# First masks of an attention layer made beside the layer before, three late tiles, and parts between two kinds of matmul

## The chip, the core and the metric

The kernel runs on one core of a Trainium2 chip. A core has five engines with an instruction queue each: TensorE (PE in the profile: matmuls and transposes, with its weight loads shown apart as PEld), VectorE (DVE), ScalarE (ACT), GpSimd (POOL) and SyncE (SP, which here only starts transfers). Each engine works through its queue in the order in which the program issued to it, and waits where an instruction needs something that is not there yet. The metric is the time of the whole program on the device in microseconds, the median of several runs.

## The reference

There are 2708 nodes with 256 features, `x`, and a matrix `adj` of 2708 x 2708. Two layers follow each other, each ending in x = layernorm(x + layer(x)).

```
# layer 0, S = adj
R = S + I, its rows scaled to sum 1
for n in 0, 1:                       # Xf = Xa = X at the start
    A  = top_p_attention(Xa)         # softmax of bilinear scores, kept to 0.9 of its mass
    Xf = R @ Xf ;  Xa = A @ Xa
    Z += Xf @ U1[n].T + Xa @ U2[n].T
layer0 = layernorm(X + Z) * ln_g + ln_b

# layer 1, 4 heads of 64
Wh  = x @ W[h]
e   = leaky_relu(s_i + s_j, 0.2)     # s_i, s_j: Wh with two vectors per head
att = softmax over j of e where adj != 0 or i == j
layer1 = att @ Wh, heads side by side
```

## The kernel before, in words

The nodes are cut into 22 tiles: tiles 0 to 15 have 128 rows, tiles 16 to 21 have 110. All matmuls are in float32.

**Layer 0** (`fast_layer0`) goes through the tiles twice (`step`, s = 0 and 1). For each target tile t, `weigh` turns the attention weights `e` in six groups of up to four tiles (`turned`: transposes by TensorE into a PSUM tile `tr`, a copy by ScalarE into `eT`) and multiplies them with the values into the PSUM tile `att`. After each group `between` is called. It scales the result into `xa` after the last group (L1030), and it calls `slot`, which lets the generators that are under way go on by one part each: the search for the kept weights of a later tile (`search`, mostly VectorE), the walk with `adj` (`walks`, TensorE, L901, with blocks `blk` of `adjT` in three buffers of `adjp`), and `finish`. In the second step `finish(t)` collects the terms of a tile (L974 on VectorE, L976 on ScalarE, L979 to L982 on GpSimd); then `norms` makes the two layernorms and `sources` what layer 1 needs of the tile as a source: transposes (L160), a copy, a matmul with the layer's weights (L166), and by ScalarE the exponentials `sb` and `tj` and the values `cs`, which are stored to DRAM as `vd[t]`. In `norms`, L129 to L137 are `layernorm` on VectorE, with the power -1/2 on GpSimd (L135); the multiplication with `g_sb` and the addition of `xt` (L187, L188) are GpSimd's.

The last four tiles, 18 to 21 (`LATE = 4`), end late, and layer 1 does not need them at once as sources. Their norms and sources are left to layer 1: the generator `prepared(t)`, which uses `layernorm_beside` (L145 to L153): three ScalarE passes and four small GpSimd operations for each norm.

**Layer 1** (`layer1`) takes the target tiles in three groups (`spans`: 8, 8 and 6 tiles, that is 1024, 1024 and 660 targets). For each group all 22 source tiles j are gone through in pairs; in the first group in the order `first`: 8 to 17, 0 to 7, 18 to 21. For one source tile

- `mask` starts the load of `v[j]` (only in the first group, L1290) and calls `neighbours`: a block of `adjT` (up to 128 x 1024) is fetched by SP into one of the three buffers of `adjp`, ScalarE makes zeros and ones of it with two passes (Sign, L1221, and Square, L1222), and where j is among the group's targets VectorE sets the diagonal (L1225);
- `weights` makes four products by VectorE, one for each head (`pt`, L1302), from the targets' terms, `tj` and the mask; there are three sets of buffers for them (`DEEP = 3`);
- `values` multiplies them with `v` into four PSUM accumulators (L1313), and `denominators` with `sb` into two more (L1323).

The loop runs over pairs of source tiles. For each it calls, in this order: `beside`, `weights` and `mask` of a later tile, `values` of both tiles, `denominators` of both, `beside` again (not in a group's last pair), `weights` and `mask` of another later tile. This order is the order of the engines' queues; SP alone is ordered by the framework. `beside` lets each late part go on by one step: the four `prepared` generators, started two calls apart, then `verdict` (checks of the fast path, some 20 small VectorE operations), then the parts of the last group's results (`settle`). At i = 11 it shares the next group's target terms.

The line numbers of the profile are those of this kernel.

Of the kernel before, what the change touches and what calls it, by code (L numbers as in the profile page):

```python
# [44 lines left out]
def kernel(  # L45
# [68 lines left out]
    g_sb = const.tile([P, D], F32, name="g_sb")  # L114
    b_sb = const.tile([P, D], F32, name="b_sb")

    LATE = 4
    x_late = const.tile([P, LATE, D], F32, name="x_late")
    engines = {nc.tensor.engine, nc.scalar.engine, nc.vector.engine, nc.gpsimd.engine}

# [57 lines left out]
            )  # L178
        queue.dma_start(vd[t][:m], vt[:m])  # L179

    def norms(t, xt, norm=layernorm, other=None):

        m = rows[t]
        hh = xe[:m, t, 0:D]
        h2 = hh if other is None else other()[:m]
        yield from norm(h2, hh, m)
        nc.gpsimd.tensor_mul(h2, h2, g_sb[:m])  # L187
        nc.gpsimd.tensor_add(h2, h2, xt[:m])  # L188
        yield
        yield from norm(hh, h2, m)  # L190
        yield
        if t < NT - LATE:
            yield

    GT = 8
    spans = [list(range(g, min(g + GT, NT))) for g in range(0, NT, GT)]
# [20 lines left out]
    def spread(g, r):  # L217

        lines = shared[g].rearrange("(t h) m -> h t m", h=H)
        n = len(spans[g]) * rows[spans[g][0]]  # L220
        for k in range(2):
            for h in range(2):
                nc.sync.dma_start(
                    r[k][:, h, :n].rearrange("p (t m) -> p t m", t=len(spans[g])),
                    lines[2 * k + h].partition_broadcast(P),
                )

    def room(pool):

# [295 lines left out]
    def fast_layer0(ep, adjp):  # L525
# [461 lines left out]


        going, doing, unfinished, stored = [], [], set(), set()
        ready, held = {}, {}  # L990
        stream = walks()
        owed = [0]
# [17 lines left out]
                    break  # L1010

        def step(s, cur, spend):
            first = None
            for t in range(NT):
                m = rows[t]
                e, rden = ready[t]
                ac = ps_at.tile([P, CHUNK], F32, name="att")
                if s == 0 and t == NT - 1:
                    next(stream)
                if s and t == NT - 2:  # L1020
                    share(0, ps_tr.tile([P, 4, P], F32, name="tr"))
                if s and t == NT - 1:
                    ahead.extend(room(ep))
                    spread(0, ahead)

                def between(n):
                    last = n == len(groups) - 1
                    if last:
                        xa = heldp.tile([P, D], F32, name="xa1")
                        nc.scalar.activation(xa[:m], ac[:m, :D], AF.Copy, scale=rden)  # L1030
                        if s and t in c3:
                            nc.gpsimd.dma_start(c3[t][:m], xa[:m])
                            stored.add(t)
                        elif s:
                            held[t] = xa
                        else:
                            doing.append(after_attention0(t, xa))
                    slot(spend[n], (s, t + 3) if n == len(groups) - 2 else None)

                def turn_next(n):  # L1040
                    u = t + n // len(groups)
                    if u == NT:
# [3 lines left out]
                first = weigh(  # L1046
                    ac[:m, :D], first or turn_next(0), m,
                    lambda j: cur[: rows[j], j, 0:D], turn_next, between,
                )
                ready.pop(t)  # L1050
# [131 lines left out]
            )  # L1182

        l0.close()
        return ahead, verdict

# [1 line left out]

    def layer1(ep, adjp, r=None, verdict=None):
        l1 = ExitStack()

        pp, rp, pj, keep = (
# [7 lines left out]
        first = list(range(GT, NT - LATE)) + list(range(GT)) + list(range(NT - LATE, NT))  # L1204


        v = {}
        for t in reversed(first):
# [1 line left out]

        def aux():
            return ps_u.tile([P, H, P], F32, name="aux")

        def neighbours(g, j):

            k = rows[j]
            i0, i1 = off[spans[g][0]], off[spans[g][-1] + 1]
            bar = adjp.tile([P, NT - HT, P], F32, name="blk")
            bar = bar.rearrange("p t d -> p (t d)")[:k, : i1 - i0]
            nc.sync.dma_start(bar, adjT[off[j] : off[j + 1], i0:i1])  # L1220
            nc.scalar.activation(bar, bar, AF.Sign)  # L1221
            nc.scalar.activation(bar, bar, AF.Square)  # L1222
            if j in spans[g]:
                own = bar[:, off[j] - i0 : off[j + 1] - i0]
                nc.vector.tensor_tensor(own, own, ident[:k, :k], op=ALU.max)  # L1225
            return bar

        def settle(g, t, val, den, u, last):

# [56 lines left out]
        def mask(n):  # L1286
            if n < len(order):
                g, _, j = order[n]
                if g == 0:
                    nc.scalar.dma_start(  # L1290
                        v[j][: rows[j]].rearrange("p h o -> p (h o)"), vd[j][: rows[j]]
                    )
                masks[n] = neighbours(g, j)

        def weights(n):
            if n < len(order):
# [32 lines left out]

        def prepared(t):  # L1330

            yield from norms(
                t, x_late[:, t - NT + LATE, :], layernorm_beside,
                lambda: pp.tile([P, D], F32, name="h2", bufs=4),
            )
            yield from sources(t, pp, aux, nc.scalar)


        late = []
        if verdict:  # L1340
            late += [[2 * k, prepared(NT - LATE + k)] for k in range(LATE)]
            late.append([2 * LATE, verdict(aux)])
        rest, running = [], []
        def beside(g, i):

            for part in list(late):
                if part[0] > 0:
                    part[0] -= 1
                elif next(part[1], late) is late:
                    late.remove(part)  # L1350
            for part in list(running):
                if next(part, running) is running:
# [17 lines left out]
        for n in range(0, len(order), 2):  # L1370
# [103 lines left out]
```

## Time and profile before

| what | value |
|---|---|
| median of 3 runs | 1587.1 us (1586.86 to 1587.92) |
| the profiled execution's own time | 1586.25 us |
| its span in the profile | 1584.4 us |
| TensorE busy | 1537.4 us, 97% |
| VectorE busy | 1201.2 us, 76% |
| ScalarE busy | 799.5 us, 50% |
| GpSimd busy | 440.9 us, 28% |
| last matmul of layer 0's attention (L258) ends | 1221.1 us from the span's start |
| first matmul of layer 1's values (L1313) begins | 1225.2 us |
| end of the first group of layer 1 (its last L1323) | about 1359.6 us |

A row of the timeline gives the start in microseconds from the span's start, the length, engine, line, operation, the output and inputs by the program's names, their shapes and the number of instructions that were merged; in brackets how long the engine stood idle before it, and what ended that. A `MATMUL` in float32 shows as two instructions. "Busy" of TensorE contains some overlap of matmuls that follow each other, so the distance from one start to the next is the better measure of what a group costs.

### The profile page before, as it was taken

The page shows a single profiled execution, that of the slowest core. Times are in us where ns is not written, and L with a number is a line of the kernel's source. Part 1 is how long each engine was busy: PE and PEld are TensorE (multiplying, and loading weights), DVE is VectorE, ACT ScalarE, POOL GpSimd, SP SyncE. Part 2 cuts the span into 40 slices and gives each one's busy share as a digit, 9 for nine tenths or more (in the row PEclk, how much of TensorE's full clock was granted, in tenths as well). Part 3 has the DMA queues.
Part 4 walks back from the last instruction along what each step waited for, and adds up shares of the span by engine and source line. Part 5 has one row for each costly group of instructions (what it writes and reads, how often), then busy time and mean ns, then how long its engine had stood idle before and what let it go on. Part 6 is the DMA issues. An engine that isn't in the chain of part 4 may idle for free. (4 is left out here: it accounts for less than half of the span.)

```text
span 1584.4 us, 23826 instructions
## 1 busy us (share of the span) xinstructions
PE 1537.4 (97%) x8029; PEld 1036.2 (65%) x8029; DVE 1201.2 (76%) x3651; ACT 799.5 (50%) x1462; POOL 440.9 (28%) x884
## 2 busy tenths in 40 slices
PE   8999999999998999999999999999998989999994
PEld 4477777776776888787778788887786323333342
DVE  4686776777309767877779888888883888999895
ACT  3444444444345455555645566656643454456473
POOL 2200000100023122232223544444541750044133
PEclk9999999999999999999999999999999999999998
DMA  6100000000144333332333444333343335334231
GB/s 163 61 12 13 9 13 9 9 11 11 43 114 105 100 84 102 80 89 72 85 89 95 110 109 109 104 99 93 91 101 110 110 110 161 95 107 133 81 100 43
DMA packets 172495, 128.27 MB, mean 81 GB/s; under 512 B 44342, under 2 KB 161804, under 8 KB 172362
## 3 DMA queue, kind: packets, MB, share of 16 engines
q1 hardware_dynamic: 162000, 111.86, 26.4%
q0 software_dynamic: 3648, 9.26, 1.7%
q10 hardware_dynamic: 6714, 5.54, 1.1%
q8 instruction: 65, 1.06, 0.3%
q14 instruction: 68, 0.56, 0.1%
HBM read 111.78 MB, written 13.46 MB: 79 GB/s over the span
## 5 line engine op out<-in xcount | busy, mean ns | idle before, releaser
L245 ACT COPY eT<-tr 128x512 f32<-128x512 f32 (+5 forms) x264 | 141.3, 535 | 287.5 <-PE tr L240 284.9
L686 ACT ACTIVATE junk<-e,minus,rth 128x2708 bf16<-128x2708 f32 (+1 forms) x88 | 232.8, 2646 | 36.1 <-POOL rth L718 35.2
L258 PE MATMUL att<-xm,eT 128*128 128x256 f32 (+3 forms) x968 | 230.9, 380 | 0.4 <-ACT xa L1030 0.4
L258 PE MATMUL att<-ba,eT 128*128 128x256 f32 (+3 forms) x968 | 230.8, 379 | 0.3 <-ACT eT L245 0.2
L901 PE MATMUL walk<-xe,blk 128*128 128x257 f32 (+3 forms) x968 | 225.3, 384 | 5.0 <-DVE xf L915 5.0
L901 PE MATMUL walk<-xm,blk 128*128 128x256 f32 (+3 forms) x968 | 222.0, 380 | 1.0 <-DVE xw L974 1.0
L1313 PE MATMUL acc<-pt,v 128*64 128x512 f32 (+3 forms) x1056 | 213.7, 548 | 4.5 <-DVE pt L1302 4.1
L901 PEld LDWEIGHTS walk<-xe,blk 128*128 128x128 f32 (+3 forms) x968 | 178.5, 187 | 50.3 <-issue 12.6
L1302 DVE SCALAR_TENSOR_TENSOR pt<-e,tj,blk 128x1024 f32<-128x1024 f32 (+3 forms) x176 | 185.5, 1122 | 20.7 <-ACT blk L1222 16.0
L901 PEld LDWEIGHTS walk<-xm,blk 128*128 128x128 f32 (+3 forms) x968 | 177.7, 186 | 34.4 <-issue 4.9
L258 PEld LDWEIGHTS att<-xm,eT 128*128 128x128 f32 (+3 forms) x968 | 169.6, 186 | 22.1 <-ACT xa L1030 0.8
L258 PEld LDWEIGHTS att<-ba,eT 128*128 128x128 f32 (+3 forms) x968 | 169.5, 186 | 22.0 <-ACT eT L245 0.8
L665 ACT ACTIVATE e<-lg 128x1024 f32<-128x1024 f32 (+1 forms) x132 | 121.0, 921 | 110.6 <-PE lg L661 107.0
L1313 PEld LDWEIGHTS acc<-pt,v 128*64 128x64 f32 (+1 forms) x1056 | 74.7, 137 | 132.9 <-issue 109.4
L766 DVE MAX8 cand<-e 128x8 f32<-128x170 f32 (+1 forms) x352 | 89.6, 324 | 90.5 <-ACT e L665 90.4
L240 PEld LDWEIGHTS tr<-ident,e 128*128 128x128 f32 (+3 forms) x968 | 115.1, 138 | 56.3 <-issue 21.0
L240 PE MATMUL tr<-ident,e 128*128 128x128 f32 (+3 forms) x968 | 147.1, 271 | 0.7 <-ACT xe L952 0.3
L1302 DVE SCALAR_TENSOR_TENSOR pt<-r,tj,blk 128x1024 f32<-128x1024 f32 (+1 forms) x88 | 109.8, 1312 | 6.1 <-PE acc L1323 3.2
L1323 PE MATMUL acc<-pt,sb 128*32 128x512 f32 (+3 forms) x1056 | 106.8, 545 | 0.0
L766 DVE MAX8 cand<-scr 128x8 f32<-128x97 f32 (+1 forms) x616 | 102.3, 246 | 0.0
L915 DVE TENSOR_TENSOR xf<-walk,xe 128x257 f32<-128x257 f32 (+1 forms) x22 | 9.4, 426 | 110.6 <-PE walk L901 110.6
L784 DVE MAX8 top<-work 128x8 f32<-128x128 f32 (+3 forms) x242 | 82.4, 340 | 8.3
(237 smaller groups left out, 1966.9 us busy)
## 6 DMA issues: line engine op xcount, KB each, us to landing
blk<-in_adjT_dram SPq DMA_DIRECT2D x32, 704.0 KB
blk<-in_adjT_dram SPq DMA_DIRECT2D x32, 512.0 KB
blk<-in_adjT_dram SPq DMA_DIRECT2D x48, 330.0 KB
blk<-in_adjT_dram SPq DMA_DIRECT2D x32, 320.0 KB
blk<-in_adjT_dram SPq DMA_DIRECT2D x12, 605.0 KB
blk<-in_adjT_dram SPq DMA_DIRECT2D x12, 440.0 KB
blk<-in_adjT_dram SPq DMA_DIRECT2D x18, 283.6 KB
c<-cs POOLq DMA_DIRECT2D x32, 128.0 KB, 2.0
```

The lines of the kernel that those rows point to most:

```text
L240: nc.tensor.transpose(tr[: rows[t], q, :m], e[:m, off[t] : off[t + 1]], ident[:m, :m])
L245: copy(eT[:k, : len(grp), :m], tr[:k, : len(grp), :m])
L258: nc.tensor.matmul(acc, eT[: rows[t], q, :m], value(t), start=(t == 0), stop=(t == NT - 1),)
L665: nc.scalar.activation(halves[:m, :, c0 : c0 + w], lg[:m, :, :w], AF.Exp, accum_out=zp[:m, n : n + 1],)
L686: nc.scalar.activation(junk[:m], e[:m], func, scale=rth, bias=minus1[:m], accum_out=acc)
L766: nc.vector.max(cand[:, n, :], src[:m, n * size : min(N, (n + 1) * size)])
L784: nc.vector.max(top[:, k : k + 8], work if k else flat)
L901: nc.tensor.matmul(ac[:m, :w], blk[: rows[j], j - j0, :m], cur[: rows[j], j, 0:w], start=(j == 0), stop=(j == NT - 1),)
L915: nc.vector.tensor_add(xf[:m], ac[:m, : D + 1], xe[:m, t, :])
L1302: nc.vector.scalar_tensor_tensor(pt[:k, :gw], targets[g][h // 2][:k, h % 2, :gw], tj[:k, j, h : h + 1], bar, op0=ALU.max, op1=ALU.mult,)
L1313: nc.tensor.matmul(acc[h // 2][c][q * FO : (q + 1) * FO, :w], v[j][:k, h, :], probs[n][h][:k, c0 : c0 + w], **at,)
L1323: nc.tensor.matmul(acc[2][c][h * 32 : (h + 1) * 32, :w], sb[:k, j, h : h + 1].to_broadcast([k, 32]), probs[n][h][:k, c0 : c0 + w], **at,)
```

## The change

- `LATE` is 3: tile 18 is finished in layer 0 like the tiles before it, with `layernorm` on VectorE; `first` becomes 8 to 18, 0 to 7, 19 to 21.
- `norms` serves the early tiles alone. For the three late tiles `prepared` writes its own norms: the statistics, the epsilon, the column `nb` and also the multiplication with `g_sb` and the addition on VectorE, one operation on GpSimd (`pow`), one pass on ScalarE. Two calls of `beside` with nothing to do lie between `pow` and `nb`. One tile takes 12 calls instead of 8.
- `neighbours` moves to the outer function, and in the second step of layer 0, at the last tile after the last but one group, the first two masks of layer 1 are made (`early`). In `mask` they are then taken as they are.
- The loads of the first three `v[j]` are started on SP instead of ScalarE's queue.
- The second call of `beside` in a pair comes between `values` and `denominators`.
- `verdict` starts after 26 calls of `beside` (`NT + 4`) instead of 8, that is in the second group.

```diff
-    LATE = 4
+    LATE = 3
...
-    def norms(t, xt, norm=layernorm, other=None):
+    def norms(t, xt):
 
         m = rows[t]
         hh = xe[:m, t, 0:D]
-        h2 = hh if other is None else other()[:m]
-        yield from norm(h2, hh, m)
-        nc.gpsimd.tensor_mul(h2, h2, g_sb[:m])
-        nc.gpsimd.tensor_add(h2, h2, xt[:m])
+        yield from layernorm(hh, hh, m)
+        nc.gpsimd.tensor_mul(hh, hh, g_sb[:m])
+        nc.gpsimd.tensor_add(hh, hh, xt[:m])
         yield
-        yield from norm(hh, h2, m)
+        yield from layernorm(hh, hh, m)
         yield
-        if t < NT - LATE:
-            yield
+        yield
...
+    first = list(range(GT, NT - LATE)) + list(range(GT)) + list(range(NT - LATE, NT))
+
+    def neighbours(g, j, adjp):
+
+        k = rows[j]
+        i0, i1 = off[spans[g][0]], off[spans[g][-1] + 1]
+        bar = adjp.tile([P, NT - HT, P], F32, name="blk")
+        bar = bar.rearrange("p t d -> p (t d)")[:k, : i1 - i0]
+        nc.sync.dma_start(bar, adjT[off[j] : off[j + 1], i0:i1])
+        nc.scalar.activation(bar, bar, AF.Sign)
+        nc.scalar.activation(bar, bar, AF.Square)
+        if j in spans[g]:
+            own = bar[:, off[j] - i0 : off[j + 1] - i0]
+            nc.vector.tensor_tensor(own, own, ident[:k, :k], op=ALU.max)
+        return bar
...
+                    if s and (t, n) == (NT - 1, len(groups) - 2):
+
+                        early.extend(neighbours(0, j, adjp) for j in first[:2])
                     slot(spend[n], (s, t + 3) if n == len(groups) - 2 else None)
...
-                    nc.scalar.dma_start(
+                    (nc.sync if n < DEEP else nc.scalar).dma_start(
                         v[j][: rows[j]].rearrange("p h o -> p (h o)"), vd[j][: rows[j]]
                     )
-                masks[n] = neighbours(g, j)
+                masks[n] = early[n] if n < len(early) else neighbours(g, j, adjp)
...
         def prepared(t):
 
-            yield from norms(
-                t, x_late[:, t - NT + LATE, :], layernorm_beside,
-                lambda: pp.tile([P, D], F32, name="h2", bufs=4),
-            )
+            m = rows[t]
+            xt = x_late[:m, t - NT + LATE, :]
+            hh = xe[:m, t, 0:D]
+            h2 = pp.tile([P, D], F32, name="h2", bufs=LATE)[:m]
+            for src, dst in ((hh, h2), (h2, hh)):
+                if src is h2:
+                    nc.vector.tensor_mul(h2, h2, g_sb[:m])
+                    nc.vector.tensor_add(h2, h2, xt)
+                st = small.tile([P, 6], F32, name="ln_st")[:m]
+                mv = small.tile([P, 2], F32, name="ln_mv")[:m]
+                ve, rs, nb = (small.tile([P, 1], F32, name=f"ln_{k}")[:m] for k in ("ve", "rs", "nb"))
+                nc.vector.bn_stats(st, src)
+                nc.vector.bn_aggr(mv, st)
+                nc.vector.tensor_scalar(ve, mv[:, 1:2], LN_EPS, None, op0=ALU.add)
+                nc.gpsimd.tensor_tensor(rs, ve, minus_half[:m], op=ALU.pow)
+
+                yield
+                yield
+                yield
+                nc.vector.tensor_scalar(nb, mv[:, 0:1], rs, -1.0, op0=ALU.mult, op1=ALU.mult)
+                yield
+                nc.scalar.activation(dst, src, AF.Identity, scale=rs, bias=nb)
+                yield
             yield from sources(t, pp, aux, nc.scalar)
 
         late = []
         if verdict:
             late += [[2 * k, prepared(NT - LATE + k)] for k in range(LATE)]
-            late.append([2 * LATE, verdict(aux)])
+            late.append([NT + 4, verdict(aux)])
...
+            if not last:
+                beside(g, i + 1)
             for u in (n, n + 1):
                 denominators(u)
             if last:
...
                 rest = [(g, t, val, den) for t in spans[g]]
-            else:
-                beside(g, i + 1)
             weights(n + 3)
             mask(n + 4)
```

`early` is handed from `fast_layer0` to `layer1`; a local variable `first` in `step` is renamed.

More of the change, by code (lines that the diff above doesn't have):

```diff
@@ L989, in fast_layer0 @@
         going, doing, unfinished, stored = [], [], set(), set()
+        early = []
         ready, held = {}, {}
@@ L1012, in step @@
         def step(s, cur, spend):
-            first = None
+            turned_first = None
             for t in range(NT):
@@ L1044, in turn_next @@
                     return turned(ready[u][0], rows[u], n % len(groups), tpp, ps_tr, nc.scalar.copy)
-                first = weigh(
-                    ac[:m, :D], first or turn_next(0), m,
+                turned_first = weigh(
+                    ac[:m, :D], turned_first or turn_next(0), m,
                     lambda j: cur[: rows[j], j, 0:D], turn_next, between,
@@ L1184, in fast_layer0, with layer1 @@
         l0.close()
-        return ahead, verdict
-    def layer1(ep, adjp, r=None, verdict=None):
+        return ahead, verdict, early
+    def layer1(ep, adjp, r=None, verdict=None, early=()):
         l1 = ExitStack()
@@ L1202, in layer1 @@
         ps_v = l1.enter_context(tc.tile_pool(name="ps_v", bufs=1, space=PSUM))
-        first = list(range(GT, NT - LATE)) + list(range(GT)) + list(range(NT - LATE, NT))
         v = {}
@@ L1212, in aux @@
             return ps_u.tile([P, H, P], F32, name="aux")
[L1214 to L1226, printed above, removed]
         def settle(g, t, val, den, u, last):
```

## The prediction, made before the change was built

> **What bounds the kernel now.** I read the shares of busy time first, then the instructions of TensorE in order of time from the end of the last attention, then the other engines over the same stretch, to see what TensorE waits for.
>
> ```profile
> PE 1537.4 (97%) x8029; PEld 1036.2 (65%) x8029; DVE 1201.2 (76%) x3651; ACT 799.5 (50%) x1462; POOL 440.9 (28%) x884
> ```
>
> TensorE is busy for 1537 of 1584.4 us, so only its gaps are to be won. TensorE in order of time (start, length, line, operation, count, idle time before it and who ended it):
>
> ```profile
> 1218.35 2.75 PE L258 MATMUL att<-ba,eT 110*110 110x256 f32 x12
> 1225.22 10.30 PE L1313 MATMUL acc<-pt,v 128*64 128x512 f32 x32 [4.11 <-DVE pt L1302]
> 1235.45 3.64 PE L1323 MATMUL acc<-pt,sb 128*32 128x512 f32 x32
> ...
> 1249.61 9.21 PE L1313 MATMUL acc<-pt,v 128*64 128x512 f32 x32
> ...
> 1273.25 1.14 PE L166 MATMUL aux<-wx,xT 128*110 128x264 f32 x4
> 1276.58 0.41 PE L160 MATMUL aux<-ident,xe 110*128 110x110 f32 x2 [2.19 <-ACT xe L153]
> 1276.92 7.09 PE L1313 MATMUL acc<-pt,v 110*64 110x512 f32 x32
> 1283.94 3.64 PE L1323 MATMUL acc<-pt,sb 110*32 110x512 f32 x32
> 1287.51 1.14 PE L166 MATMUL aux<-wx,xT 128*110 128x264 f32 x4
> 1290.86 0.41 PE L160 MATMUL aux<-ident,xe 110*128 110x110 f32 x2 [2.21 <-ACT xe L153]
> ```
>
> An undisturbed pair of source tiles costs 10.59 us: 7.02 of values and 3.57 of denominators (1276.92, 1283.94, 1287.51). Layer 1 loses time at three kinds of place: 4.11 us before its first matmul, a first pair (10.23 instead of 7.02) and a third pair (9.14) that are too long, and 2.2 us, three times, between a late tile's L166 and the next one's L160 (the third, 2.10, is before L160 at 1305.14). After 1317 TensorE has no such gap until the end. VectorE, ScalarE and GpSimd beside it:
>
> ```profile
> 1223.88 24.01 DVE L1302 SCALAR_TENSOR_TENSOR pt<-e,tj,blk 128x1024 f32<-128x1024 f32 x20 [11.34 <-ACT blk L1222]
> 1251.96 15.39 DVE L1302 SCALAR_TENSOR_TENSOR pt<-e,tj,blk 128x1024 f32<-128x1024 f32 x12 [4.07 <-ACT blk L1222]
> 1267.92 10.59 DVE L1302 SCALAR_TENSOR_TENSOR pt<-e,tj,blk 110x1024 f32<-110x1024 f32 x8 [0.57 <-ACT blk L1222]
> ```
>
> ```profile
> 1218.61 0.34 ACT L245 COPY eT<-tr 110x220 f32<-110x220 f32 x1 [1.39 <-PE tr L240]
> 1221.14 0.47 ACT L1030 ACTIVATE xa<-att,rden 110x256 f32<-110x256 f32 x1 [2.19 <-PE att L258]
> 1221.70 1.06 ACT L1221 ACTIVATE blk<-blk 128x1024 f32<-128x1024 f32 x1
> 1222.79 1.06 ACT L1222 ACTIVATE blk<-blk 128x1024 f32<-128x1024 f32 x1
> ...
> 1248.89 0.60 ACT L153 ACTIVATE h<-xe,lb_nb,lb_rs 110x256 f32<-110x256 f32 x1 [9.39 <-POOL lb_nb L151]
> ```
>
> ```profile
> 1234.98 12.96 POOL L149 TENSOR_SCALAR lb_sq<-lb_sq 110x1 f32<-110x1 f32 x1 [6.13 <-ACT h L148]
> ```
>
> The first product waits for its mask, which ScalarE makes after `xa`. From 1223.88 VectorE makes 20 products at 1.20 us each with no pause: eight per pair, 9.6 us, against TensorE's 10.59, so it has 1 us to spare per pair once level, and in the first pair it is the pace (last values 11.57 after the first product). L149 ends only when that run of VectorE ends; ScalarE's L153 stood behind it, the next mask behind L153: that is the third pair's delay.
>
> **The change, part by part** (against the profiled execution: 1586.25 us, span 1584.4, 0.85 below the median of 1587.1).
>
> *Masks made early.* ScalarE does four mask passes after its last `eT` copy, at 1218.95: the first mask is ready 2 x 1.07 later, at 1221.1, when the last attention matmul ends. The product then starts 2.78 us sooner relative to that end: **-2.8**. Its other needs are there: masks 0 and 1 were fetched at 1195 and 1204, the targets' copies were issued at 1200.5, and by the order and sizes of the pools the first eight products lie where `xm` and `qT` were, last read at 1212.5. The two fetches move ahead in the program but take the same buffers, which the walks free, so SP issues them (0.36 each) when it does now. What queues behind the passes on ScalarE: `xa` slips from 1221.14 to about 1223.2, and with it GpSimd's L981 and L982 (0.72 each), which now run beside products. By the pools' order one accumulator takes `att`'s bank; it is first written 5.3 us after the first product, after `xa`. If a target or buffer is late the gain is nothing: +2.8.
>
> *Three v loads on SP*, 0.3 us of issue each, behind fetches that wait for buffers anyway. The first pair is paced by VectorE, so v may land 2 us late for nothing: 0.
>
> *Tile 18 goes back into layer 0.* TensorE's L160 and L166 cost 0.19 and 0.89 there (start to start at 1180.16 and 1186.35, tile 17), 0.34 and 1.07 in layer 1: **-0.3**. VectorE gains 2 x (0.85 + 0.41) us and a wait for GpSimd of up to 1.5; its idle 4.08 us before L974 at 1195.23 hides that, and `e` of the last tile is ready at 1202.4, 2.2 us before its use: 0, at worst +1.
>
> *Parts between values and denominators.* The next tile's L160 stood right behind L166, waiting for ScalarE (sb, tj, s_src, four cs, a store, L153: 2.14 us). Now 3.57 us of denominators lie between: **-6.5** (2.19 + 2.21 + 2.10). In groups 1 and 2 only `share` changes place on TensorE.
>
> *Norms.* Four GpSimd operations and three ScalarE passes per norm become one GpSimd `pow` and one pass; ScalarE's Identity now follows VectorE's `nb`, three calls after `pow`, so no mask stands behind a late GpSimd: the third pair's delay goes, **-2.1**. VectorE pays: bn_stats, bn_aggr and the epsilon 0.85 (the same three at 1155.09), `nb` 0.2 (as L743, a column by a column, 0.21), multiply and add 0.42 each (as L974). By the product that ends the sixth pair: 48 products at 1.20 = 57.6, six norm starts 5.1, four `nb` 0.8, three multiply-adds 2.5, together 66.0; three matmuls of 0.44 (7.02 us are 16) follow: 67.3 us after the first product. TensorE alone would be there at 11.57 + 3.57 + 4 x 10.59 + 0.34 + 7.02 = 64.9. So VectorE is the bound for the first six pairs: **+2.5**. Afterwards L166 gives it time back.
>
> The unknown is what GpSimd beside it costs. Bounds: 0 (20 products at 1.20 with L146 and L149 in the run) and 7.2 (40 products at 1.32, as the eight at 1267.92, 4.8; four `nb` waiting 0.6 for their `pow`, 2.4). I take **+1.5**, nearest to the 12 products of 15.39 us, where some ten GpSimd operations cost 0.9; here there are eight, two of them wide.
>
> [...]
>
> *Verdict later.* 3.9 us of VectorE move to group 1's third to seventh pair, where VectorE idles 0.4 to 0.8 us per pair and products may be 2.6 late: 0, at worst +1.6.
>
> Sum: -2.8 - 0.3 - 6.5 - 2.1 + 2.5 + 1.5 = **-7.7**, so 1587.1 - 7.7 = 1579.4 us.
>
> **Rivals.**
> A. GpSimd and VectorE hold each other up at the upper bound: 5.7 us dearer, gain 2.0, 1585.1 us. For it: 1.32 us products around 1270. Against: most of GpSimd's work leaves.
> B. The early masks do nothing, because the first product waits for something that the mask hid until now: gain 4.9, 1582.2 us. For it: nothing shows what else ended before 1223.88. Against: the buffers and fetches above.
> C. Slower: GpSimd is shut out as in the L149 of 12.96 us, and VectorE's waiting at `nb` does not let it in. L981 is asked for 2 us after the first product, L982 and the six `pow` queue behind it at p us each, so the last `pow` ends at 2 + 8p; its `nb` is due at 73, with products behind it on VectorE and TensorE behind these. At 12.96 us that is 33 late: 1612.1 us. It costs from p = 8.9 on and makes the kernel slower than before, beyond what can be told, from 10.3 (11 late). For it: one row. Against: that row ended with VectorE's run, and at `nb` VectorE stands still.
>
> **How the numbers follow.** Forecast 0.57, A 0.18, B 0.15, C 0.10. Measurement tells 0.2%, 3.2 us, from no change. Faster by that: the forecast, B and a third of A, 0.78; within it: the rest of A, 0.12; slower: C, 0.10. The forecast's own range is 1577 (no GpSimd cost, some VectorE work in its idle moments) to 1582; with A and B it reaches 1576 to 1586.
>
> **What would show it.** First product within 0.5 us of the last attention matmul's end and TensorE's gap there 1.3 instead of 4.1; no wait before L160; VectorE without a pause from there until about 67 us later, with short waits of TensorE on products in the fourth to sixth pair; `pow` under 2 us or waits at `nb` under 1; VectorE's products in the stretch at 1.20 to 1.25. Wrong it would be by a late target, a GpSimd backlog, or TensorE waiting in layer 0's last tile.

## The result

The changed kernel takes 1575.88 us (median of 4 runs, 1575.84 to 1576.54) against 1587.34 us (4 runs, 1586.86 to 1587.92): 11.5 us less. The ratio is 0.9929, 95% interval 0.9911 to 0.9946. Forecast were 1579.4 us, in a range of 1576.0 to 1586.0.

The profiled execution of the changed kernel took 1576.54 us, its span is 1574.7 us; against the 1584.4 us of before that is 9.7 less. Line numbers move: L1302 is now L1305 (products), L1313 L1316 (values), L1323 L1326 (denominators), L258 L273 (last attention), L1221 and L1222 L236 and L237 (mask passes), L981 and L982 L996 and L997; the new norms are L1341 to L1356.

TensorE in order of time, after (the columns are those of before):

```profile
1220.45 2.76 PE L273 MATMUL att<-ba,eT 110*110 110x256 f32 x12
1225.87 10.07 PE L1316 MATMUL acc<-pt,v 128*64 128x512 f32 x32 [2.66 <-DVE pt L1305]
1235.88 3.64 PE L1326 MATMUL acc<-pt,sb 128*32 128x512 f32 x32
...
1250.03 7.09 PE L1316 MATMUL acc<-pt,v 128*64 128x512 f32 x32
...
1260.62 8.12 PE L1316 MATMUL acc<-pt,v 128*64 128x512 f32 x32
...
1272.24 7.85 PE L1316 MATMUL acc<-pt,v 110*64 110x512 f32 x32
...
1283.93 7.71 PE L1316 MATMUL acc<-pt,v 110*64 110x512 f32 x32
1291.57 1.14 PE L166 MATMUL aux<-wx,xT 128*110 128x264 f32 x4
...
1292.76 3.64 PE L1326 MATMUL acc<-pt,sb 110*32 110x512 f32 x32
1296.33 0.41 PE L160 MATMUL aux<-ident,xe 110*128 110x110 f32 x2
```

The gap ahead of the first values is 2.66 instead of 4.11 us, the third pair takes 7.09 instead of 9.21, and L160 follows without a wait. New are three pairs of 8.12, 7.85 and 7.71 us. VectorE and GpSimd beside it:

```profile
1223.30 10.59 DVE L1305 SCALAR_TENSOR_TENSOR pt<-e,tj,blk 128x1024 f32<-128x1024 f32 x8 [8.68 <-PE att L273]
...
1234.56 9.65 DVE L1305 SCALAR_TENSOR_TENSOR pt<-e,tj,blk 128x1024 f32<-128x1024 f32 x8
```

```profile
1225.57 0.79 POOL L996 TENSOR_TENSOR xe<-xe,xa 110x256 f32<-110x256 f32 x1 [9.27 <-ACT xa L1046]
1226.32 1.70 POOL L997 TENSOR_TENSOR x_late<-x_late,b_sb 110x256 f32<-110x256 f32 x1
1234.72 1.52 POOL L1349 TENSOR_TENSOR ln_rs<-ln_ve,minus_half 110x1 f32<-110x1 f32 x1 [6.69 <-DVE ln_ve L1348]
```

The first product starts 0.09 us after the last attention matmul (2.77 before). The eight products beside L996 and L997 take 1.32 us each, the next eight, beside a `pow`, 1.20.

The two profiled executions side by side, in microseconds:

| stretch | before | after | difference |
|---|---|---|---|
| span's start to the 26th matmul | 13.25 | 13.48 | +0.23 |
| from there to the end of the last attention matmul | 1207.86 | 1209.73 | +1.87 |
| from there to the end of the last matmul | 343.17 | 333.86 | -9.31 |
| from there to the span's end | 20.10 | 17.62 | -2.48 |
| span | 1584.4 | 1574.7 | -9.7 |

The third row is the sum of: first product -2.68, first pair +1.01 (11.57 to 12.58 from first product to last values), third pair -2.12, three waits before L160 -6.50, tile 18's L160 and L166 gone from layer 1 -1.41, pairs four to six +2.41; that makes -9.29. The last row but one was nowhere in my sum.

### The profile page after: what moved, and what is told of

Read it like the earlier page. It is cut to its first block, busy times and chain, and to the rows that moved or that the text cites. A ratio compares the mean times of both kernels' runs of the same rounds, so it can differ in the third digit from the quotient of the medians.

```text
span 1574.7 us, 23765 instructions
## 1 busy us (share of the span) xinstructions
PE 1537.8 (98%) x8029; PEld 1037.3 (66%) x8029; DVE 1207.8 (77%) x3689; ACT 791.7 (50%) x1428; POOL 407.6 (26%) x853
## 4 chain that ended last, share of the span: by engine, by line
PE 92%; DVE 4%; POOL 1%; ACT 1%; issue 1%; DMA 0%; ACTq 0%; POOLq 0%; DVEq 0%
PE att L273 25%; PE walk L916 24%; PE acc L1316 13%; PE lg L676 7%; PE acc L1326 7%; PE tr L255 6%; PE tr L961 2%; PE tr L975 2%; PE tr L646 1%; PE tr L166 1%; DVE scr L766 1%; DVE scr L847 0%; DVE cand L781 0%; DVE e L850 0%; PE aux L1236 0%
## 5 line engine op out<-in xcount | busy, mean ns | idle before, releaser
L273 PE MATMUL att<-xm,eT 128*128 128x256 f32 (+3 forms) x968 | 230.9, 380 | 0.4 <-ACT xa L1046 0.4
L273 PE MATMUL att<-ba,eT 128*128 128x256 f32 (+3 forms) x968 | 230.8, 379 | 0.3 <-ACT eT L260 0.2
L1316 PE MATMUL acc<-pt,v 128*64 128x512 f32 (+3 forms) x1056 | 214.3, 551 | 2.7 <-DVE pt L1305 2.7
L1305 DVE SCALAR_TENSOR_TENSOR pt<-e,tj,blk 128x1024 f32<-128x1024 f32 (+3 forms) x176 | 184.2, 1112 | 12.7 <-PE att L273 8.7
L273 PEld LDWEIGHTS att<-xm,eT 128*128 128x128 f32 (+3 forms) x968 | 169.6, 186 | 22.1 <-ACT xa L1046 0.8
L273 PEld LDWEIGHTS att<-ba,eT 128*128 128x128 f32 (+3 forms) x968 | 169.5, 186 | 22.0 <-ACT eT L260 0.8
L1316 PEld LDWEIGHTS acc<-pt,v 128*64 128x64 f32 (+1 forms) x1056 | 75.7, 138 | 132.0 <-issue 107.8
L1305 DVE SCALAR_TENSOR_TENSOR pt<-r,tj,blk 128x1024 f32<-128x1024 f32 (+1 forms) x88 | 109.8, 1310 | 3.0 <-PE acc L1326 1.3
L1326 PE MATMUL acc<-pt,sb 128*32 128x512 f32 (+3 forms) x1056 | 106.8, 545 | 0.0
L236 ACT ACTIVATE blk<-blk 128x1024 f32<-128x1024 f32 (+3 forms) x66 | 63.3, 958 | 83.5 <-DMA blk<-in_adjT_dram 63.3
```

The lines of the kernel that those rows point to most:

```text
L273: nc.tensor.matmul(acc, eT[: rows[t], q, :m], value(t), start=(t == 0), stop=(t == NT - 1),)
L1305: nc.vector.scalar_tensor_tensor(pt[:k, :gw], targets[g][h // 2][:k, h % 2, :gw], tj[:k, j, h : h + 1], bar, op0=ALU.max, op1=ALU.mult,)
L1316: nc.tensor.matmul(acc[h // 2][c][q * FO : (q + 1) * FO, :w], v[j][:k, h, :], probs[n][h][:k, c0 : c0 + w], **at,)
L1326: nc.tensor.matmul(acc[2][c][h * 32 : (h + 1) * 32, :w], sb[:k, j, h : h + 1].to_broadcast([k, 32]), probs[n][h][:k, c0 : c0 + w], **at,)
```

## The experiments

Every kernel was timed in at least five executions beside the kernel before on the same chip, whose median lay at 1586.7 to 1587.4 us. The stretches of the table above are called seam (last attention matmul to last matmul) and tail (last matmul to the span's end) here. The expectations of the two runs on GpSimd's last branch count the tail from the last matmul's start, which adds 0.3 us. In the code, cuts are marked by `...`.

### The parts behind the denominators again

```diff
-            if not last:
-                beside(g, i + 1)
             for u in (n, n + 1):
                 denominators(u)
             if last:
                 ...
                 rest = [(g, t, val, den) for t in spans[g]]
+            else:
+                beside(g, i + 1)
             weights(n + 3)
```

> The changed kernel with one thing undone: the second round of parts of a pair is called behind the denominators again. With three late tiles two L166 then stand right ahead of the next tile's L160 (tile 19 to 20, 20 to 21). My theory: two waits of 2.1 to 2.2 us before L160 come back, the last matmul is 4.3 us later, 1580.2 us. Rival, that the 6.5 us were won because fewer tiles are late or because the norms are faster: no wait before L160, 1575.9 us.

Measured: 1582.83 us, 6.95 more than the changed kernel. TensorE:

```profile
1297.70 0.41 PE L160 MATMUL aux<-ident,xe 110*128 110x110 f32 x2 [2.38 <-ACT xe L1356]
1298.04 8.78 PE L1316 MATMUL acc<-pt,v 128*64 128x512 f32 x32
...
1313.68 0.41 PE L160 MATMUL aux<-ident,xe 110*128 110x110 f32 x2 [2.21 <-ACT xe L1356]
1314.02 7.09 PE L1316 MATMUL acc<-pt,v 128*64 128x512 f32 x32
```

The two waits are back, 4.59 us together, as expected: the denominators were the cover, and three late tiles instead of four account for the third wait. The pair behind the first wait takes 1.69 us longer, which no theory had. The busy time by stretch shows why; the column behind the five engines is TensorE's granted clock:

```profile
1298.50:1301.90 3.40, 3.40 (x10) 0.98 (x8) 2.46 (x5) 3.34 (x5) 0.00 (x0) 0.50 0.64 202
```

Only ten matmul instructions ran in this stretch, which the clock's record gives as 3.413 us at half clock from 1298.5: 1.7 us lost. More on this below.

### Without the early masks

```diff
-                        early.extend(neighbours(0, j, adjp) for j in first[:2])
+                        early.extend(neighbours(0, j, adjp) for j in first[:0])
```

> The changed kernel with the list of early masks left empty, so the first masks are made in layer 1, behind xa. My theory: the first product starts 2.7 us later after the last attention matmul, but GpSimd's two wide additions (L996, L997) then run before the products, which take 1.20 instead of 1.32 us, 1.0 us less for the eight; together +1.7, 1577.6 us. Rival 1, the additions are not what slows the eight products: +2.7, 1578.6 us. Rival 2, something else holds the first product: 0, 1575.9 us.

Measured: 1575.77 us, seam 333.78: no difference, which is rival 2 by its number. But nothing else held the product; the masks were early all the same. ScalarE of this run:

```profile
1210.63 1.06 ACT L236 ACTIVATE blk<-blk 128x1024 f32<-128x1024 f32 x1 [3.12 <-DMA blk<-in_adjT_dram]
1211.72 1.06 ACT L237 ACTIVATE blk<-blk 128x1024 f32<-128x1024 f32 x1
...
1216.52 1.06 ACT L236 ACTIVATE blk<-blk 128x1024 f32<-128x1024 f32 x1 [0.35 <-DMA blk<-in_adjT_dram]
...
1222.26 0.47 ACT L1046 ACTIVATE xa<-att,rden 110x256 f32<-110x256 f32 x1 [2.25 <-PE att L273]
```

Two masks are made ahead of `xa`, although the code issues `xa` in layer 0 and these masks in layer 1. Between the layers the framework had put ScalarE's instructions in another order than the code's; that SP alone is ordered by the framework, as is said ahead of the prediction, does not hold across the seam. What remained in the diff to allow that were the three v loads on SP. The kernel before has its first v load on ScalarE's queue right behind `xa`, and ahead of the first mask pass at 1221.70:

```profile
1221.15 0.35 ACTq L1290 DMA_DIRECT2D v<-v  x1
```

### The v loads, alone and undone

Undone in the changed kernel, and done alone in the kernel before:

```diff
-                    (nc.sync if n < DEEP else nc.scalar).dma_start(
+                    nc.scalar.dma_start(
```

> The changed kernel with the first three v loads on ScalarE's queue again; the early masks stay. Theory since the run without early masks: what held the masks was ScalarE's own v load, which waits for the last attention matmul and had the mask passes behind it; the change took it away twice, by moving the loads and by issuing two masks ahead of them. Then the first product still starts within 0.3 us of the last attention matmul, 1575.8 us. Rival, the moved loads alone did it: the product starts 2.8 us after, 1578.5 us.

```diff
-                    nc.scalar.dma_start(
+                    (nc.sync if n < DEEP else nc.scalar).dma_start(
```

> The kernel before with one line changed, the first three v loads issued by SP instead of ScalarE. Theory: masks and first product no longer wait behind a v load, the product starts 2.7 us sooner after the last attention matmul, 1584.2 us with the medians so far (1586.9 before); the first pair may lose up to 1.0 of it, as L981 and L982 then run beside the products, 1585.2 us. Rival, issuing the masks early is needed as well: 1586.9 us.

Measured: 1575.64 us for the first, with the product 0.09 us after the attention; 1584.23 us for the second, with the same 0.09. Either of the two measures takes the 2.7 us away, so one of them is superfluous. The execution in the profile of the second took 1585.5 us, the longest of its eleven, with a window at half clock in layer 1. For the moved loads alone the profile shows a price ahead of the seam (1209.14 instead of 1207.86 us to the last attention matmul; 0.94 of it is a wait of TensorE at 1213.33 for a copy `eT`, among which the mask passes now lie), and one line that I had not foreseen:

```profile
1222.40 51.71 DVE L1302 SCALAR_TENSOR_TENSOR pt<-e,tj,blk 128x1024 f32<-128x1024 f32 x40 [9.86 <-PE att L258]
```

Forty products without a pause: the stall of the third pair is gone, though the norms are the old ones. The median is the expected one, but partly by luck: beside the -2.7 of the first product, the profile has -2.1 for the third pair, against +1.3 ahead of the seam, +0.9 in the first pair and +1.7 at half clock.

### The old norms in the changed kernel

```diff
-            for src, dst in ((hh, h2), (h2, hh)):
-                ...
+            yield from layernorm_beside(h2, hh, m)
+            nc.gpsimd.tensor_mul(h2, h2, g_sb[:m])
+            nc.gpsimd.tensor_add(h2, h2, xt)
+            yield
+            yield from layernorm_beside(hh, h2, m)
+            yield
             yield from sources(t, pp, aux, nc.scalar)
```

> The changed kernel with the late tiles' norms as they were before (ScalarE's sums, four GpSimd operations, the product and the sum on GpSimd); three late tiles, the moved loads and the new place of the parts stay. By my prediction's step, the old norms shut a GpSimd operation out and stall the third pair: third pair 9.1 instead of 7.1 us, and pairs four to six 7.1 instead of 8.18, 7.84 and 7.71, from the last attention matmul to the last matmul 333.5 instead of 333.8 us. Rival, since the kernel before with only the loads moved no longer had that stall: third pair 7.1 too, 331.4 us, so that the new norms are a loss of 2.4. In both, GpSimd has some 24 more instructions ahead of its branch, so the tail may be 20.0 instead of 17.6 us: 1575.6 to 1578.0 us in the first case, 1573.5 to 1575.9 in the second.

Measured: 1574.31 us (five runs, 1573.84 to 1574.76), seam 331.77, tail 17.9. The rival holds. Pairs three to six:

```profile
1249.45 7.09 PE L1330 MATMUL acc<-pt,v 128*64 128x512 f32 x32
...
1260.38 7.09 PE L1330 MATMUL acc<-pt,v 128*64 128x512 f32 x32
...
1272.38 7.09 PE L1330 MATMUL acc<-pt,v 110*64 110x512 f32 x32
...
1284.38 7.09 PE L1330 MATMUL acc<-pt,v 110*64 110x512 f32 x32
```

The second GpSimd operation of `layernorm_beside`, the one of 12.96 us in the profile of before, is here:

```profile
1234.81 1.01 POOL L163 TENSOR_SCALAR lb_sq<-lb_sq 110x1 f32<-110x1 f32 x1 [6.12 <-ACT h L162]
```

So the new norms cost 2.4 us of VectorE and won nothing in these executions: as far as the third pair goes, the gain belongs to whatever keeps that operation from being shut out, that is, from ending only when VectorE's run of products ends. This version is 1.6 us faster than the changed kernel, by medians from different series (ratio to before 0.9918, interval 0.9904 to 0.9931).

### Four late tiles

```diff
-    LATE = 3
+    LATE = 4
```

> The changed kernel with four late tiles again. My theory: layer 0 gets back 1.1 us of tile 18's two TensorE groups and 0.5 of waiting for VectorE, so the last attention matmul is 1.6 us sooner; layer 1 pays 1.4 for the groups and, with one tile's norm more on VectorE ahead of the bound, up to 2.9: 1575.9 - 1.6 + 4.3 = 1578.6 us. Rival, VectorE's work for the fourth tile falls behind the bound: + 1.4 alone, 1575.7 us.

Measured: 1576.38 us. Up to the last attention matmul 1207.88 us, 1.85 less than with three late tiles; seam 336.37, 2.5 more, of which 1.4 are tile 18's groups and 1.1 the bound (fourth, fifth and sixth pair 8.18, 8.60 and 8.10). Between theory and rival: VectorE's work for a fourth tile falls partly behind the bound. With the new norms, moving tile 18 is worth about 0.5 us, by medians from different series.

### GpSimd's bias first

```diff
-            nc.gpsimd.tensor_add(xt, xt, held.pop(t)[:m])
             nc.gpsimd.tensor_add(ca[:m], ca[:m], b_sb[:m])
+            nc.gpsimd.tensor_add(xt, xt, held.pop(t)[:m])
```

> The changed kernel with GpSimd's L997 (bias onto the residual, which needs nothing late) exchanged with L996 (which waits for xa), so that only L996 runs beside the first eight products. Theory: GpSimd's wide additions cost VectorE about 0.5 us each there; the eight products take 10.1 instead of 10.59 us and, as VectorE is the pace until the sixth pair, 0.5 us are won, 1575.3 us. Rival, one wide addition is enough for the whole loss: 10.59 and 1575.8 us.

Measured: 1575.18 us, seam 333.34 instead of 333.86.

```profile
1222.68 10.12 DVE L1305 SCALAR_TENSOR_TENSOR pt<-e,tj,blk 128x1024 f32<-128x1024 f32 x8 [8.67 <-PE att L273]
```

10.12 instead of 10.59: a wide GpSimd addition costs VectorE's products about 0.5 us, and two cost 1.0.

### Norms later

```diff
-                yield
                 yield
                 yield
                 nc.vector.tensor_scalar(nb, mv[:, 0:1], rs, -1.0, op0=ALU.mult, op1=ALU.mult)
...
-            late += [[2 * k, prepared(NT - LATE + k)] for k in range(LATE)]
+            late += [[4 + 2 * k, prepared(NT - LATE + k)] for k in range(LATE)]
```

> The changed kernel with the late tiles' norms begun four calls later and one call less between the power and its use, so that more of their VectorE work falls behind the sixth pair. Theory that VectorE is the pace until there: pairs four to six take 7.02 us of values each instead of 8.05, 7.78 and 7.64, no wait before L160, 2.4 us won, 1573.4 us. Rival, the same VectorE work then makes later pairs wait: 1575.8 us.

Measured: 1581.12 us, 5.2 more than the changed kernel. The pairs did as the theory said, and then something new went wrong:

```profile
1259.97 7.09 PE L1316 MATMUL acc<-pt,v 128*64 128x512 f32 x32
...
1270.55 7.09 PE L1316 MATMUL acc<-pt,v 110*64 110x512 f32 x32
...
1281.14 7.20 PE L1316 MATMUL acc<-pt,v 110*64 110x512 f32 x32
...
1309.85 0.53 PE L160 MATMUL aux<-ident,xe 110*128 110x110 f32 x2 [4.80 <-ACT xe L1355]
1310.31 8.60 PE L1316 MATMUL acc<-pt,v 128*64 128x512 f32 x32
```

ScalarE and SP of this run tell where the 4.80 us come from:

```profile
1305.64 1.06 ACT L236 ACTIVATE blk<-blk 128x1024 f32<-128x1024 f32 x1 [12.79 <-DMA blk<-in_adjT_dram]
1306.72 1.06 ACT L237 ACTIVATE blk<-blk 128x1024 f32<-128x1024 f32 x1
1307.69 0.15 ACT L170 ACTIVATE sb<-aux 110x4 f32<-110x4 f32 x1
```

```profile
1290.83 6.56 SPq L221 DMA_DIRECT2D r<-shared  x4
1297.48 21.16 SPq L235 DMA_DIRECT2D blk<-in_adjT_dram  x5
```

SP issued the four copies of the next group's targets (512 KB each) and only then the next mask's fetch, at 1297.48; the mask was there at 1305.6. ScalarE stood before it for 12.79 us with the source parts of L166 behind it, and L160 needs what follows these. In the changed kernel there was a fetch between SP's store of the shared terms and the copies (1295.76). A window at half clock followed the wait here as well; it is the likely source of the 1.51 us that the pair behind it takes beyond 7.09.

### Norms later, copies apart

The two edits above together, and the copies issued one per call:

```diff
-                spread(g + 1, targets[g + 1])
+                running.append(spread_slowly(g + 1, targets[g + 1]))
+                next(running[-1])
```

> The run with norms later and with L996 and L997 exchanged, together, and the four copies of the next group's targets issued one per call instead of all at once, so that no mask fetch stands behind four of them on SP. Theory: the new wait of the run with norms later (a mask fetch behind the copies, ScalarE's source parts behind that mask) goes, no wait of TensorE before L160, pairs three to six 7.09 us each: 2.4 less than the exchange alone, from the last attention matmul to the last matmul 330.9 us, 1572.8 us. Rival, a fetch is late however the copies are spread: L160 waits 1 us or more and 1575.2 us or more.

Measured: 1575.04 us, seam 333.66. The third to sixth pair took 7.09 to 7.21 us, the seventh 8.01, and L160 still waited 1.59 us behind a mask whose block came only at 1302.06. So the rival holds, near its 1575.2 us. VectorE's work could be moved out of the bound, but then a fetch beside the copies was late again: it was issued at 1292.91, between the second and the third copy. How much of its 9 us the copies cost was not separated.

### The place of GpSimd's last branch

```diff
             layer1_weights()
+            idle = small.tile([P, 1], F32, name="idle")
+            for _ in range(40):     # 98 in the kernel before
+                nc.gpsimd.memset(idle, 0.0)
             step(0, xm, [0] * len(groups))
```

> The changed kernel with 40 memsets of one column on GpSimd in layer 0, where it idles; they only move the place of GpSimd's later instructions. [...] Rival, that the tail is shorter for what layer 1 leaves behind: 17.9 and 1575.9 us.

> [...] Rival, the tail does not hang on the place of the code: 20.4 and 1587.3 us.

The changed kernel has 30 GpSimd instructions fewer than the kernel before; its 40 memsets make that 10 more and were meant to bring the long tail back, the 98 in the kernel before to take it away. Measured: 1577.76 us with a tail of 20.02, and 1584.31 us with a tail of 17.60. So it went, both ways, and neither rival holds. From the trace's records of GpSimd (time, duration, operation; the branch jumps over the code for the general case, which these inputs do not need):

```
before             1573.82 0.045 COMPARE_BRANCH   1576.76 EVENT_SEMAPHORE   1576.85 6.685 DRAIN
after              1566.61 0.045 COMPARE_BRANCH   1567.08 EVENT_SEMAPHORE   1567.18 6.685 DRAIN
after, 40 more     1565.31 0.045 COMPARE_BRANCH   1568.20 EVENT_SEMAPHORE   1568.28 6.685 DRAIN
before, 98 more    1574.10 0.045 COMPARE_BRANCH   1574.57 EVENT_SEMAPHORE   1574.65 6.685 DRAIN
```

From the branch to the next instruction it is 2.9 us or 0.47 us, a difference of 2.4. The 6.685 us drain follows, and the span ends soon after it. Other traces fit: with as many GpSimd instructions as before it is 3.16 us (before, v loads on SP), with seven fewer 0.48 (old norms). That the place of the code decides is thus shown: counted from the kernel before, the wait is there at 0 and 10 instructions more, and gone at 30 and 7 fewer and at 98 more. Why at these places was not shown, nor what is waited for. Instruction transfers of 8192 bytes run at that time in all four traces, but the records do not say for which engine, and in the profiles of before and after one begins 0.2 us behind the branch alike, with the wait and without it. Thirty GpSimd instructions fewer happened to take the wait away; it has nothing to do with what the change is about.

### Old norms, four late tiles, bias first

```diff
-    LATE = 3
+    LATE = 4
...
-            for src, dst in ((hh, h2), (h2, hh)):
+            yield from layernorm_beside(h2, hh, m)
...
+            nc.gpsimd.tensor_add(ca[:m], ca[:m], b_sb[:m])
             nc.gpsimd.tensor_add(xt, xt, held.pop(t)[:m])
-            nc.gpsimd.tensor_add(ca[:m], ca[:m], b_sb[:m])
...
+            for _ in range(98):
+                nc.gpsimd.memset(idle, 0.0)
```

> [...] From the runs: TensorE up to the last attention matmul 1.8 us shorter, as with four late tiles (1207.9 instead of 1209.7), from there to the last matmul 331.8 + 1.4 for tile 18's groups - 0.5 for the exchange = 332.7, tail 17.6 to 17.9: 0.9 less than the version with old norms alone, 1573.4 us. Rival, a fourth tile's old norm brings back a stall of a pair or a wait before L160 (2.1 us each): 1575.5 us or more.

This version has the old norms, four late tiles, L996 and L997 exchanged, and 98 memsets on GpSimd like the kernel before in the run on its last branch. Measured: 1573.92 us median, but in two kinds: 1573.68, 1573.80, 1573.92 and 1577.09, 1577.28. The profiled execution is the one of 1577.28, and its third pair is the 9.21 us of the kernel before, for the same reason:

```profile
1232.84 12.71 POOL L163 TENSOR_SCALAR lb_sq<-lb_sq 110x1 f32<-110x1 f32 x1 [7.58 <-ACT h L162]
```

Another pair of that execution took 9.15 us behind a late mask fetch; the two stalls, 4.2 us, are about the distance from the expected seam (336.50 against 332.7). The spans of the three short executions, 1571.8 to 1572.1, are 3.3 to 3.6 us less, which is what the expectation had; they have no trace, but going by their lengths alone the expectation came true in three executions and the rival in two. On this evidence, which is one trace and five lengths, the old norms are a risk of 2 to 4 us rather than a fixed cost, and the new norms buy it off for 2.4. Neither this version nor the one before it is clearly the better: 1573.92 with two executions above 1577, and 1574.31 with none.

## Why the prediction was right, and where it was not

The direction and most of the size were right: the terms of the sum came to -7.4 us where I had -7.7. But the kernel gained 11.5 and came out 0.12 us below the range, and two of the causes that I named are not, or not alone, the causes. That the sum fits so well is partly luck: tile 18 came out 0.7 us dearer and GpSimd 0.5 us cheaper than I had put down. Of the rivals, A (7.2 us for GpSimd beside VectorE) and C (8.9 us or more for each operation of GpSimd) fell by the rows: 1.01 us in all, and 1.45 to 5.23 us for each `pow`. B, that the first product waits for something else than its mask, did not come true either, as the product did start 0.09 us after the attention.

**Masks made early (-2.8).** Measured -2.68. The size is right, the cause is only half right. The delay was ScalarE's queue: a v load ahead of the masks. The early list removes it, and so does moving the v loads, each without the other. I had called the v loads worth 0, and had read the code's order across the seam as ScalarE's order, where the framework had made its own. TensorE's gap became 2.66 and not the 1.3 that I gave as a sign; the first values wait for `xa` or v, and VectorE paces that pair anyway.

**Tile 18 back in layer 0 (-0.3).** Measured +0.44: -1.41 in layer 1, +1.85 ahead of the seam. TensorE's groups cost there the 1.08 that I had put down; the failed step is "its idle 4.08 us hides that". It hid it there, but not earlier, where the walk's matmuls of a tile wait until VectorE has read the finished result of the tile before (L989):

```profile
1181.28 4.14 PE L916 MATMUL walk<-xm,blk 128*110 128x256 f32 x18 [0.53 <-DVE xw L989]
```

All nine traces of kernels with three late tiles have this wait, 0.30 to 0.53 us, and none of the five with four. The groups and this wait make 1.61 of the 1.85 us; the rest is not accounted for. That the move still pays with the new norms is due to the 1.1 us that a fourth late tile adds to VectorE's bound.

**Parts between values and denominators (-6.5).** Measured -6.50. Undoing it alone brought back 4.59 us at the two places where L160 then follows L166 at once; the third such place went with the fourth late tile.

**Norms: third pair (-2.1).** Measured -2.12, but with the old norms it was gone as well in two versions (loads moved in the kernel before, old norms in the changed one), and there again in the one with four late tiles and the bias first. The step that failed is "the third pair's delay goes" as a consequence of the norms. What decides whether L149 or its like (L163 in the versions with old norms) is shut out for 12.7 to 13.0 us or ends after 0.85 or 1.01 us is open. In all of these VectorE ran its products without a pause at that time. While the operation was shut out, VectorE kept to 1.20 to 1.22 us a product; where it was let in, products took 1.29 on average (36 in 46.45 us, 40 in 51.71).

**Norms: VectorE as the bound (+2.5).** Measured +2.41, by pairs of 8.12, 7.85 and 7.71 us. Confirmed twice, by beginning later (7.09, 7.09, 7.20) and by leaving the work off VectorE (7.09 each).

**GpSimd beside VectorE (+1.5, bounds 0 and 7.2).** Measured +1.01, all of it from L996 and L997, half a microsecond each. `pow` lasted 1.5 us, once 5.23, and cost VectorE nothing that shows. (Of the row that I took as nearest, 12 products in 15.39 us, the cost beside 1.20 each is 1.0 and not 0.9.)

**Verdict later (0).** No wait appeared in group 1.

**The tail.** Not in the sum: -2.48, from the place of a branch. It could not have been taken from the profile's rows, but the tail's 20 us were on the path in plain sight, and I asked of no number there whether the change touched it.

**The clock.** Also missing in the sum is what a TensorE wait of 2 us does afterwards. The records of the granted clock show windows of 3.413 us, or two in a row, at half speed. Here are those of seven traces up to the last matmul (start, length); of the other seven, two more have the one at the seam, and none has a later one:

```
before             508.0 (3.4 us)   1224.8 (3.4)
before, 98 more    505.2 (3.4)      1222.0 (6.8)   1276.6 (3.4)
before, v on SP    507.9 (3.4)      1224.7 (3.4)   1289.6 (3.4)
parts behind       506.6 (3.4)                     1298.5 (3.4)
norms later        507.9 (3.4)      1224.7 (3.4)   1310.0 (3.4)
after              508.3 (3.4)      1225.1 (6.8)
old norms          507.6 (3.4)
```

The window near 508 is in every trace. The one near 1225 follows the gap at the seam and costs nothing, as VectorE paces that pair: the seam is 333.86 us with it and 333.78 without. The last column follows a wait before L160, and there it costs 1.5 to 1.7 us: this is the pair of the kernel before with 98 memsets, against 7.09 us of the same pair in the first profile of that kernel, and the stretches around it.

```profile
1275.18 0.41 PE L160 MATMUL aux<-ident,xe 110*128 110x110 f32 x2 [2.19 <-ACT xe L153]
1275.51 8.79 PE L1316 MATMUL acc<-pt,v 110*64 110x512 f32 x32
```

```profile
1272.00:1276.60 4.60, 2.41 (x12) 1.14 (x14) 4.60 (x4) 2.71 (x13) 4.52 (x4) 1.00 0.45 138
1276.60:1280.00 3.40, 3.40 (x10) 0.96 (x8) 1.74 (x7) 3.37 (x8) 1.96 (x6) 0.50 0.66 188
1280.00:1284.40 4.40, 4.40 (x24) 1.31 (x24) 4.40 (x4) 1.88 (x2) 4.24 (x4) 1.00 0.11 37
```

The medians differ by 11.5 us, the two profiled executions by 9.7. Of these 1.8 us, 1.1 are the profiled execution of before (1586.25 us) lying below its median, and 0.7 that of after (1576.54) lying above its own. The first has a mean granted clock of 0.993, and 44 of the 52 later executions of that kernel had 0.990, so the clock may have a part in it. It is not shown, as those executions have no trace; and the three later ones with 0.993 (1586.07, 1586.40 and 1586.38 us) lie only 0.5 to 0.9 us below the medians of their series.

Waits of 2.19 to 2.38 us were followed by a window at half clock in three of these runs, and others of the same length were not.

Which of them were can be read from the traces. The window near 508 sets the place of all others, one every 3.413 us (before and after alike, the one near 1225 begins 716.80 us behind it, 210 times 3.4133), and in each one can add up the time in which TensorE ran no matmul. From 14 us to the last matmul of all fourteen traces, 24 windows at full clock had 1.99 us or more of it, and all 24 were followed by one at half clock. Of the windows at full clock with 1.84 us or less none was, though some forty of these had 1.0 us or more. Between them lie two, both at the seam: one with 1.89 us was followed (after), one with 1.93 was not (v loads on ScalarE again). So a wait of 2.2 us costs about 1.7 more where it falls almost whole into one window (2.0 us of it in "before, 98 more" and in "before, v on SP"), and nothing more where it is split, as in the first profile (1.61 and 0.58 us). That is a rule of these traces, found afterwards and not tested by a run of its own.

## What to carry to other kernels

A wait of the bounding engine is paid for twice if its clock follows its activity: price the removal of a 2 us wait with what the clock does in the microseconds after it (here 1.5 to 1.7 us more), and look at the granted clock of more than one execution, since the place of its window differs from trace to trace (here the one near 508 us began at 505.2 to 508.3). When two edits of a change aim at one delay, ask of each alone which queue it clears; the cheaper one, here one word in a DMA's queue, may do all of it. And where one engine's slack is filled by work taken from another, look at what its lateness had been keeping apart: here fetches and copies on SP that came together as soon as VectorE's norms were moved.

## What the runs showed of the hardware that I had not expected

- A taken branch on GpSimd cost 2.9 us in some kernels and 0.47 in others, and 30 or 40 instructions more or less, hundreds of microseconds earlier, decide it; what it waits for was not shown.
- TensorE's clock halves for 3.413 us after a wait of only 2.2 to 2.4 us, in some executions and not in others: 1.7 us each time that TensorE is the bound. What decides is how much of the wait falls into one of the clock's windows: 1.99 us and more always did it in these traces, 1.84 us and less never.
- One and the same small GpSimd operation beside VectorE's products took 0.85 and 1.01 us in two versions and 12.7 to 13.0 us in three; one of these three kernels has executions of two lengths, 3.2 us or more apart. What decides it stayed open.
